# Local attention on Trainium2: weighing values or weighing tokens

## The chip, the cores and the metric

The kernel runs on one core of a Trainium2 chip. TensorE multiplies matrices and writes to PSUM; VectorE (DVE) and ScalarE (ACT) read PSUM; GpSimd (POOL) works on SBUF only; SyncE (SP) issues the transfers. Each engine takes its instructions in order, and they wait for one another by semaphores. The metric is the device time of one execution in microseconds (us). Everything is float32.

## The reference

A linear-attention block comes first (8 sequences of 512 tokens, width 128), then six layers of local attention and feed-forward. Cut to the layers and to what the change touches:

```python
def local_attention(q, k, v):              # 16 heads of 64, windows of 32 tokens
    bk2, bv2 = look(bk), look(bv)          # the previous window and the own one: 64 keys
    sim = einsum('bhwie,bhwje->bhwij', bq, bk2) * 8.0
    sim = where(mask, -max, sim)
    attn = softmax(sim, -1)
    return einsum('bhwij,bhwje->bhwie', attn, bv2)

def attn_layer(x, Wqkv, qs, ksc, Wo):
    q, k, v = split(x @ Wqkv, 3)           # v: 128 -> 16 heads x 64
    q, k = rotary(l2norm(q) * qs), rotary(l2norm(k) * ksc)
    return merge_heads(local_attention(q, k, v)) @ Wo

def ffn_layer(x, ...):
    a, gate = split(layernorm(x) @ W1 + b1, 2)     # 128 -> 2 x 341
    return a * gelu(gate) @ W2 + b2
```

For one head h, attn_h (x Wv_h) Wo_h equals (attn_h x) (Wv_h Wo_h). The kernel before computes the left side, the changed one the right side.

## The kernel before

The work of the six layers is cut into 192 units: 6 layers x 8 sequences x 4 blocks of 128 tokens. Each sequence is held as `state[b]`, 128 features by 512 tokens. The main loop (L766) runs over turns `t`. In turn `t` one unit enters, and older units do later steps; `at(t, lag, step)` calls a step for the unit that entered `lag` turns ago. With `ends=True` a step runs only for the last block of a sequence: this is how the feed-forward part, which works on 512 tokens at once, is put into every fourth turn. Four turns, one sequence of one layer, are called a batch below.

TensorE's order is the order in which the program is written (L757, `manual_schedule`). The orders of the other engines come out of a list scheduler, which takes what is ready on its own clock, prefers what stands under `tc.high_priority()`, and obeys `issue_behind(later, earlier)`, an order on one engine without a semaphore.

The steps of a unit:

- `proj` (L439), lag 0, for queries and for keys: two 128x512 products into a PSUM tile of tag "mm"; VectorE multiplies it by the rotary tables twice (`turned` L459, `straight` L467), ScalarE squares it (L475), GpSimd adds the two products (L482).
- `sum_squares` (L484) and `unit_length` (L491), lag 0: norms on VectorE, roots on ScalarE, scaling on GpSimd (L498).
- `values` and `spread` (L502 to L530), lag 0: the value product, a copy to SBUF, and up to ten transfers that lay the 64 values of each window out over the partitions.
- `by_features` (L532), lag 1: TensorE transposes queries and keys in four groups of four, each into a PSUM tile of tag "tr", which ScalarE copies out.
- `masked` (L553) and `scores` (L563), lag 1: ScalarE writes the mask to PSUM (tag "s"), 64 small products are added to it, VectorE takes the maxima (L580), ScalarE the 16 exponentials (L584), VectorE sums and reciprocals (L590, L591).
- `by_keys` (L594), lag 2: eight transposes of the weights and two copies. `weigh_values` (L604), lag 2: 64 small products with the values, then VectorE divides (L621).
- `out_by_features` (L627), lag 2: eight transposes and two copies (L635). `out_project` (L637), lag 3: eight products with Wo, and VectorE adds the result to `state` (L647).
- Feed-forward, at the ends: `feed_norm` (lag 3), `feed_first` (lag 4), `feed_middle` (lag 5, hidden products L667 and L669, gelu L673, product L675), `feed_last` (lag 6, L702, then L711).

[...] A new tile of a tag waits until all readers of the tile that held its buffer are done. Readers on two engines of the same PSUM tile run one after the other. `nc.tensor.addr_align` (L668 and L671, and in the loop) pads TensorE's instruction stream. The layer's weights are loaded by `load_layer` (L409) when its first unit enters.

Of the kernel before, what the change touches and what calls it, by code (L numbers as in the profile page):

```python
# [15 lines left out]
P = 128  # L16
# [7 lines left out]
FILL = 16  # L24
IN_STEP = 98
# [3 lines left out]
def sandwich_kernel(ctx: ExitStack, tc: tile.TileContext, ins: dict, out: bass.AP):  # L29
# [5 lines left out]
    DEPTH = ins["L0_ffn_Wqkv"].shape[0]  # L35
# [18 lines left out]
    state = [const.tile([P, N + 1], F32, tag=f"state_{b}", name=f"state_{b}") for b in range(B)]  # L54
    for b in range(B):
        nc.vector.memset(state[b][HD:P, 0:1], 0.0)
# [16 lines left out]
    tables, exps, divisions, copies, pcopies, maxima = [], [], [], [], [], []  # L73
# [7 lines left out]
    def gelu_only():  # L81
        ld = nc.scalar.preload_act_table_set("gelu_and_others")
        issue_behind(ld, pcopies[-1])
        issue_behind(ld, exps[-1])
        tables.append(ld)
# [67 lines left out]
    tw = wl.tile([P, 3, 2, 512], F32, tag="wqkv", name="tw")  # L153
# [4 lines left out]
    nc.sync.dma_start(tw[:, 2], a_w[:, 2])  # L158
# [3 lines left out]
    woT = tw[:, 2].rearrange("p s (c d) -> p (s c) d", d=DM)  # L162
# [246 lines left out]
    def load_layer(l):  # L409
        wqkv = wl.tile([P, 3, 2, 512], F32, tag="wqkv", name=f"wqkv_{l}")  # L410
        nc.sync.dma_start(
            wqkv, ins["L0_ffn_Wqkv"][l].rearrange("p (t s c) -> p t s c", t=3, s=2)
        )
        wo = wl.tile([P, NP, DM], F32, tag="wo", name=f"wo_{l}")
        nc.sync.dma_start(wo, ins["L0_ffn_Wo"][l].rearrange("(c p) d -> p c d", p=P))
# [21 lines left out]
        return dict(wqkv=wqkv, wo=wo, w1=w1, w2=w2, tab=tab)  # L437

    def proj(u, s):  # L439

        L, b, j = u["L"], u["b"], u["j"]
        wqkv, tab = L["wqkv"], L["tab"]
# [7 lines left out]
        for a in range(2):  # L450
            nc.tensor.matmul(  # L451
                ps[:, a].rearrange("p h d -> p (h d)"), lhs, wqkv[:, s, a, :], start=True, stop=True
            )
# [12 lines left out]
        def straight():  # L466
            nc.vector.tensor_tensor(  # L467
                t1, ps,
                tab[:, 2 * s, j, :].rearrange("p (a d) -> p a d", a=2).unsqueeze(2)
                .to_broadcast([P, 2, H, HF]),  # L470
                ALU.mult,
            )

        def squared(a):
            nc.scalar.activation(sq[:, :, a, :], ps[:, a], AF.Square)  # L475
# [8 lines left out]
    def sum_squares(u, s):  # L484
        su = nc.vector.tensor_reduce(  # L485
            u["ss"][:, s], u["sq", s].rearrange("p h a d -> p h (a d)"), AX.X, ALU.add
        )
        if divisions:
            issue_behind(su, divisions[-1])
# [12 lines left out]
    def values(u):  # L502
        L, b, j = u["L"], u["b"], u["j"]
        lhs = state[b][:, j * P : (j + 1) * P]

        v0 = f3.tile([P, 2, 512], F32, tag="v0", name="v0")
        ps = psum.tile([P, 2, 512], F32, tag="mm", name="mm")
        for p in range(2):
            nc.tensor.matmul(ps[:, p, :], lhs, L["wqkv"][:, 2, p, :], start=True, stop=True)  # L509
        u["v0"], u["v0ps"] = v0, ps  # L510

    def spread(u):
        j, v0 = u["j"], u["v0"]
        cp = nc.scalar.copy(v0, u.pop("v0ps"))
        if copies:
            issue_behind(cp, copies[-1])

        v2 = f2.tile([P, 4, 512], F32, tag="v2", name="v2")
        for p in range(2):
            if j == 0:  # L520
                nc.gpsimd.memset(v2[HD * p : HD * p + W, 0, :], 0.0)
            else:
                nc.sync.dma_start(v2[HD * p : HD * p + W, 0, :], u["B"]["v0"][P - W : P, p, :])
            nc.sync.dma_start(v2[HD * p + W : HD * (p + 1), 0, :], v0[0:W, p, :])
            for w in range(1, 4):
                nc.sync.dma_start(
                    v2[HD * p : HD * (p + 1), w, :], v0[W * (w - 1) : W * (w + 1), p, :]
                )
        u["B"]["v0"] = v0
        u["v2"] = v2  # L530
# [22 lines left out]
    def masked(u):  # L553
# [7 lines left out]
        issue_behind(sd, copies[-1])  # L561

    def scores(u):  # L563
# [24 lines left out]
        exps.append(ex)  # L588
        su = f2.tile([P, NP, 2], F32, tag="su", name="su")
        nc.vector.tensor_reduce(su, pe, AX.X, ALU.add)  # L590
        nc.vector.reciprocal(su, su)  # L591
        u["pe"], u["su"] = pe, su

    def by_keys(u):  # L594
        pe = u["pe"]
        u["pT"] = pT = f1.tile([P, NP, P], F32, tag="pT", name="pT")
        for c in range(0, NP, 4):
            ps = psum.tile([P, 4, P], F32, tag="tr", name="tr")
            for i in range(4):
                transposed(ps[:, i, :], pe[:, c + i].rearrange("p a k -> p (a k)"), P, P)  # L600
            with tc.high_priority():
                pcopies.append(nc.scalar.copy(pT[:, c : c + 4, :], ps))

    def weigh_values(u):  # L604


        v2, pT, su = u["v2"], u["pT"], u["su"]
        po = psum.tile([P, 2, NP, HD], F32, tag="s", name="po", bufs=1)
        for pair in range(NP):
            for w in range(4):  # L610
                for p in range(2):
                    r = slice(HD * p, HD * (p + 1))
                    nc.tensor.matmul(  # L613
                        po[W * w : W * (w + 1), p, pair, :],
                        pT[r, pair, W * w : W * (w + 1)],
                        v2[r, w, HD * pair : HD * (pair + 1)],
                        start=(pair == 0), stop=True, skip_group_check=True,
                    )
        u["on"] = on = f1.tile([P, NP, 2, HD], F32, tag="on", name="on")
        with tc.high_priority():  # L620
            dv = nc.vector.tensor_tensor(  # L621
                on.rearrange("t c p d -> t p c d"), po,
                su.rearrange("t c p -> t p c").unsqueeze(3).to_broadcast([P, 2, NP, HD]), ALU.mult,
            )
        divisions.append(dv)

    def out_by_features(u):  # L627
        on = u["on"]
        u["oT"] = oT = f1.tile([P, NP, P], F32, tag="oT", name="oT")
        for c in range(0, NP, 4):  # L630
            ps = psum.tile([P, 4, P], F32, tag="tr", name="tr")
            for i in range(4):
                transposed(ps[:, i, :], on[:, c + i].rearrange("p a d -> p (a d)"), P, P)
            with tc.high_priority():
                nc.scalar.copy(oT[:, c : c + 4, :], ps)  # L635

    def out_project(u):  # L637

        L, b, j, oT = u["L"], u["b"], u["j"], u["oT"]
        py = psum.tile([P, P], F32, tag="s", name="py", bufs=1)  # L640
        for c in range(NP):
            nc.tensor.matmul(py, L["wo"][:, c, :], oT[:, c, :], start=(c == 0), stop=(c == NP - 1))  # L642
# [7 lines left out]
    def feed_norm(u):  # L650
# [6 lines left out]
        u["normed"] = layer_norm(f2, xn, ps, NB, by_log=True, later=True)  # L657
# [4 lines left out]
    def feed_hidden(u, c):  # L662
# [5 lines left out]
        nc.tensor.addr_align(FILL, offset=FILL // 2)  # L668
        nc.tensor.matmul(pg[:cn, 1], w1[:, c0 : c0 + cn], xnT, start=True, stop=True)  # L669
        if c < NCH - 1:  # L670
            nc.tensor.addr_align(FILL, offset=FILL // 2)  # L671
# [85 lines left out]
    with tc.manual_schedule(engines={mybir.EngineType.PE}):  # L757
# [8 lines left out]
        for t in range(len(units) + 7):  # L766
            if t < len(units):
                u = units[t]
                if u["l"] not in layers:
                    layers[u["l"]] = load_layer(u["l"])  # L770
                u["L"] = layers[u["l"]]


            gelus = 0 <= t - 5 < len(units) and units[t - 5]["j"] == NB - 1
            at(t, 0, proj, 0)
            at(t, 0, proj, 1)


            if t % NB == 1 and NB < t < len(units):
                nc.tensor.addr_align(128, offset=IN_STEP)  # L780
            if t % NB == 3 and NB < t < len(units):
                nc.tensor.addr_align(FILL)
            at(t, 2, by_keys)
            if gelus:
                gelu_only()
            at(t, 3, out_project)
# [3 lines left out]
            if t == 1:  # L790
                attn_out(B - 1)
            at(t, 1, by_features, 0)
            at(t, 2, weigh_values)
            at(t, 1, by_features, 4, 0)
            at(t, 1, masked)
            at(t, 0, values)
# [6 lines left out]
            at(t, 1, by_features, 4, 1)  # L803
            at(t, 0, spread)
            at(t, 3, feed_norm, ends=True)
            at(t, 4, feed_first, ends=True)

            ends = 9 + NB * B * (DEPTH - 1) <= t < len(units) + 5
            after = 10 + NB * B * (DEPTH - 1) <= t < len(units) + 6
            if after:  # L810
                at(t, 10, out_roots, ends=True)
            if ends:
                at(t, 9, out_by_tokens, ends=True)
                at(t, 9, out_stats, ends=True)
            at(t, 5, feed_middle, ends=True)
            if gelus:
                at(t, 0, unit_length)
            at(t, 6, feed_last, ends=True)
            at(t, 1, scores)
            if after:  # L820
                at(t, 10, store, ends=True)
            if t == len(units) + 5:
                at(t, 6, out_by_tokens)
                at(t, 6, out_stats)
# [104 lines left out]
```

## Time and profile before

| | before |
|---|---|
| median of 3 runs | 3643.95 us (3640.91 to 3646.99) |
| span of the profiled execution (all that is given of its time) | 3641.2 us |
| first projection of the layers | at 478.96 us |
| last projection of the layers | at 3561.48 us |
| TensorE busy, granted clock | 98%, 0.993 |
| VectorE, ScalarE, GpSimd busy | 77%, 76%, 51% |

The span is the time from the first to the last instruction of one profiled execution. The first 479 us are the linear attention, which the change leaves as it is but for the tile that holds one of its weights. "Busy" counts the time in which an engine runs at least one instruction; matmuls overlap, and on the quarters of TensorE's rows several run at once, so TensorE's durations are best read from the distance between starts.

### The profile page before, as it was taken

To read this page: it belongs to the slowest core of one execution; us is meant where nothing else is said; L and a number is where in the kernel's file an instruction comes from. 1 tells how busy PE (TensorE), PEld (TensorE's weight loads), DVE (VectorE), ACT (ScalarE), POOL (GpSimd) and SP (SyncE) were. 2 spreads that over 40 slices of the span, in tenths; PEclk is the share of its full clock that TensorE was granted. 3 is DMA by queue.
4 is the path that set the end of the run, shared out by engine and by line. 5 is a ranking of instruction groups with operands and counts; after the bars stand their busy time and mean duration, and the time that the engine had idled before them with its cause. 6 is when DMAs were issued, how large, how long until landed. Compare 5 with 4: busy or idle time off the path is not lost.

```text
span 3641.2 us, 153034 instructions
## 1 busy us (share of the span) xinstructions
PE 3575.2 (98%) x65184; PEld 2404.3 (66%) x65184; DVE 2796.4 (77%) x3915; ACT 2765.6 (76%) x6864; POOL 1843.6 (51%) x1311
## 2 busy tenths in 40 slices
PE   8999989999999999999999999999999999999997
PEld 4555556666766666676766766667676676766765
DVE  4555567887878788787887878878787887878885
ACT  4555557787888888888787888888878787887875
POOL 0000045555655556555565655556555565556652
PEclk9999999999999999999999999999999999999998
DMA  3121132222232222232222322223222222222221
GB/s 109 46 53 47 42 89 68 65 65 69 79 77 72 65 64 71 77 81 68 61 69 68 87 72 69 65 65 86 71 71 69 60 70 64 66 68 73 74 74 47
DMA packets 158598, 250.73 MB, mean 69 GB/s; under 512 B 33774, under 2 KB 54508, under 8 KB 157164
## 3 DMA queue, kind: packets, MB, share of 16 engines
q1 hardware_dynamic: 157932, 240.93, 25.2%
q8 instruction: 530, 8.68, 1.0%
q14 instruction: 136, 1.11, 0.1%
HBM read 41.31 MB, written 4.46 MB: 13 GB/s over the span
## 4 chain that ended last, share of the span: by engine, by line
PE 87%; ACT 9%; DVE 2%; issue 1%; DMA 1%; POOL 0%; SPq 0%; POOLq 0%; DVEq 0%; ACTq 0%
PE tr L70 19%; PE mm L451 14%; PE py L642 10%; PE mm L509 9%; PE po L613 8%; PE sp L572 6%; ACT pe L584 4%; PE mm L667 4%; PE mm L669 4%; PE y L299 3%; PE py L702 3%; PE sc L269 2%; PE po L348 2%; ACT L76 1%; PE vv L247 1%; ACT oT L635 1%
## 5 line engine op out<-in xcount | busy, mean ns | idle before, releaser
L482 POOL TENSOR_TENSOR qk<-t,t 128x1024 f32<-128x1024 f32 x384 | 910.9, 2372 | 619.1 <-DVE t L467 424.7
L498 POOL TENSOR_TENSOR qk<-qk,ss 128x1024 f32<-128x1024 f32 x384 | 722.4, 1902 | 16.0
L451 PE MATMUL mm<-wqkv,state 128*128 128x512 f32 x1536 | 700.3, 596 | 0.6 <-issue 0.6
L584 ACT ACTIVATE pe<-sp,mx 128x64 f32<-128x64 f32 x3072 | 652.0, 381 | 2.4 <-DVE mx L580 2.3
L459 DVE TENSOR_TENSOR t<-mm,tab 128x1024 f32<-128x1024 f32 x384 | 468.3, 1219 | 220.3 <-PE mm L451 214.9
L475 ACT ACTIVATE sq<-mm 128x512 f32<-128x512 f32 x768 | 420.6, 605 | 127.4 <-DVE t L467 120.9
L467 DVE TENSOR_TENSOR t<-mm,tab 128x1024 f32<-128x1024 f32 x384 | 468.1, 1219 | 5.9
L451 PEld LDWEIGHTS mm<-wqkv,state 128*128 128x128 f32 x1536 | 273.1, 190 | 289.8 <-issue 242.4
L485 DVE TENSOR_REDUCE ss<-sq 128x16 f32<-128x1024 f32 x384 | 448.4, 1209 | 0.1
L70 PE MATMUL tr<-ident,qk 128*128 128x128 f32 x3072 | 440.9, 276 | 1.8 <-ACT qT L548 0.8
L70 PEld LDWEIGHTS tr<-ident,qk 128*128 128x128 f32 x3072 | 351.3, 141 | 120.7 <-issue 56.3
L642 PE MATMUL py<-oT,wo 128*128 128x128 f32 x3072 | 379.3, 277 | 0.3 <-ACT oT L635 0.3
L642 PEld LDWEIGHTS py<-oT,wo 128*128 128x128 f32 x3072 | 368.1, 196 | 0.5 <-ACT oT L635 0.5
L509 PE MATMUL mm<-wqkv,state 128*128 128x512 f32 x768 | 362.9, 595 | 2.6 <-DVE t L467 2.6
L635 ACT COPY oT<-tr 128x512 f32<-128x512 f32 x384 | 205.5, 587 | 168.1 <-PE tr L70 165.5
L572 PEld LDWEIGHTS sp<-kT,qT 64*32 64x32 f32 x24576 | 264.2, 105 | 91.3 <-issue 54.3
L613 PE MATMUL po<-v,pT 64*32 64x64 f32 x24576 | 297.0, 225 | 9.6 <-issue 3.9
L548 ACT COPY qT<-tr 128x512 f32<-128x512 f32 x384 | 226.3, 589 | 99.6 <-PE tr L70 99.1
L613 PEld LDWEIGHTS po<-v,pT 64*32 64x32 f32 x24576 | 268.8, 105 | 46.0 <-PE tr L70 24.6
L572 PE MATMUL sp<-kT,qT 64*32 64x64 f32 x24576 | 297.6, 225 | 0.3 <-issue 0.3
L495 POOL TENSOR_SCALAR ss<-ss 128x32 f32<-128x32 f32 x192 | 54.7, 285 | 478.7 <-ACT ss L98 470.8
L548 ACT COPY kT<-tr 128x512 f32<-128x512 f32 x384 | 225.6, 588 | 74.8 <-PE tr L70 74.5
(110 smaller groups left out, 5243.9 us busy)
## 6 DMA issues: line engine op xcount, KB each, us to landing
v<-v SPq DMA_DIRECT2D x1152, 128.0 KB
v<-v SPq DMA_DIRECT2D x672, 64.0 KB
rs<-roots SPq DMA_DIRECT2D x64, 256.0 KB
wqkv<-in_L_ffn_Wqkv_dram SPq DMA_DIRECT2D x6, 1536.0 KB
wo<-in_L_ffn_Wo_dram SPq DMA_DIRECT2D x6, 512.0 KB
xin<-_attn_hidden_states_dram SPq DMA_DIRECT2D x8, 256.0 KB
xr<-_attn_hidden_states_dram SPq DMA_DIRECT2D x8, 256.0 KB
x<-xr SPq DMA_DIRECT2D x8, 256.0 KB
```

What stands on the lines that cost most here:

```text
L70: nc.tensor.transpose(ps[:cols, :rows], src, ident[:rows, :rows])
L451: nc.tensor.matmul(ps[:, a].rearrange("p h d -> p (h d)"), lhs, wqkv[:, s, a, :], start=True, stop=True)
L459: nc.vector.tensor_tensor(t2, ps[:, ::-1], tab[:, 2 * s + 1, j, :].rearrange("p (a d) -> p a d", a=2).unsqueeze(2) .to_broadcast([P, 2, H, ...
L467: nc.vector.tensor_tensor(t1, ps, tab[:, 2 * s, j, :].rearrange("p (a d) -> p a d", a=2).unsqueeze(2) .to_broadcast([P, 2, H, HF]), ALU.mult,)
L482: nc.gpsimd.tensor_tensor(qk[:, s].rearrange("p h a d -> p a h d"), t1, t2, ALU.add)
L498: nc.gpsimd.tensor_tensor(t, t, ss[:, i, :].unsqueeze(2).to_broadcast([P, H, HD]), ALU.mult)
L509: nc.tensor.matmul(ps[:, p, :], lhs, L["wqkv"][:, 2, p, :], start=True, stop=True)
L548: copies.append(nc.scalar.copy(dst, ps))
L572: nc.tensor.matmul(sp[W * w : W * (w + 1), p, pair, :], qT[HD * p : HD * (p + 1), pair, W * w : W * (w + 1)], kT[HD * p : HD * (p + 1), pa ...
L584: ex = nc.scalar.activation(pe[:, pair, p, :], sp[:, p, pair, :], AF.Exp, bias=mx[:, p, pair : pair + 1])
L613: nc.tensor.matmul(po[W * w : W * (w + 1), p, pair, :], pT[r, pair, W * w : W * (w + 1)], v2[r, w, HD * pair : HD * (pair + 1)], start=(pa ...
L642: nc.tensor.matmul(py, L["wo"][:, c, :], oT[:, c, :], start=(c == 0), stop=(c == NP - 1))
```

## The change

The values are never computed. Once a layer, the products Wv_h Wo_h are made for the 16 heads (`value_products`: 16 products of 64 rows, kept as `wm`). The host lays the weights out for this (`Wqk` and `Wvo` in place of `Wqkv` and `Wo`). For a unit:

- `by_tokens` (lag 2) transposes two 128-token windows of `state`, one shifted back by 32 tokens, and ScalarE copies them out. For this the state gets 32 columns of zeros in front.
- `divided` (lag 2): sums and reciprocals as before, but the weights themselves are divided, by GpSimd.
- `by_keys` (lag 3) is one VectorE transpose in 32x32 blocks, of 128x1024.
- `weigh_tokens` (lag 3): eight products of 32 rows by 512 columns, on four quarters of TensorE's rows, into two "mm" tiles, and two ScalarE copies of 128x1024.
- `out_project` (lag 4): 16 products in place of eight, into a "tr" tile in place of "s".

Everything behind it moves by one turn. The padding of the instruction stream goes, the loads of the next layer are issued half a layer ahead, `feed_norm` copies its transposes to SBUF before the statistics, and some orders on ScalarE and VectorE are written differently. The core of the diff:

```diff
-        wqkv = wl.tile([P, 3, 2, 512], F32, tag="wqkv", name=f"wqkv_{l}")
...
+        wqk = wl.tile([P, 2, 2, 512], F32, tag="wqk", name=f"wqk_{l}")
+        nc.sync.dma_start(wqk, ins["L0_ffn_Wqk"][l].rearrange("p (t s c) -> p t s c", t=2, s=2))
...
+    def value_weights(l):
+
+        wv = f1.tile([P, NP, DM], F32, tag="on", name="wv")
+        wo = f1.tile([P, NP, DM], F32, tag="oT", name="wo")
+        for s, t in enumerate((wv, wo)):
+            nc.sync.dma_start(t.rearrange("p c d -> p (c d)"), ins["L0_ffn_Wvo"][l, s])
+        wm = wl.tile([P, 2, NP, DM], F32, tag="wm", name=f"wm_{l}")
+        layers[l].update(wv=wv, wo=wo, wm=wm)
+
+    def value_products(l):
+        L = layers[l]
+        for c in range(0, NP, 4):
+            ps = psum.tile([P, 2, 4, DM], F32, tag="mm", name="wm")
+            for i in range(4):
+                for p in range(2):
+                    r = slice(HD * p, HD * (p + 1))
+                    nc.tensor.matmul(
+                        ps[:, p, i, :], L["wv"][r, c + i, :], L["wo"][r, c + i, :], start=True, stop=True,
+                        skip_group_check=True,
+                    )
+            nc.scalar.copy(L["wm"][:, :, c : c + 4, :], ps)
...
+    def by_tokens(u):
+
+        b, j = u["b"], u["j"]
+        ps = psum.tile([P, 2, P], F32, tag="tr", name="tx")
+        for a in range(2):
+            c0 = j * P + a * W
+            transposed(ps[:, a, :], wide[b][:, c0 : c0 + P], P, P)
+        u["x"] = x = f2.tile([P, 2, P], F32, tag="x", name="x")
+        nc.scalar.copy(x, ps)
...
         issue_behind(sd, copies[-1])
+        issue_behind(sd, squared_last[-1])
...
+    def divided(u):
+        pe = u["pe"]
         su = f2.tile([P, NP, 2], F32, tag="su", name="su")
-        nc.vector.tensor_reduce(su, pe, AX.X, ALU.add)
+        sm = nc.vector.tensor_reduce(su, pe, AX.X, ALU.add)
+        if turns:
+            issue_behind(sm, turns[-1])
         nc.vector.reciprocal(su, su)
-        u["pe"], u["su"] = pe, su
+        nc.gpsimd.tensor_tensor(pe, pe, su.unsqueeze(3).to_broadcast([P, NP, 2, 2 * W]), ALU.mult)
 
     def by_keys(u):
...
+        u["pT"] = pT = f1.tile([P, H, 2, W], F32, tag="pT", name="pT")
+        turned = nc.vector.transpose(
+            pT.rearrange("k h a t -> k (h a t)"), u["pe"].rearrange("t c p k -> t (c p k)")
+        )
+        issue_behind(turned, straights[-1])
+        turns.append(turned)
+
+    def weigh_tokens(u):
+
+        x, pT = u["x"], u["pT"]
+        ps = [psum.tile([P, 2, H, W], F32, tag="mm", name="z") for _ in range(2)]
+        for a in range(2):
             for w in range(4):
...
+                r = slice(W * w, W * (w + 1))
+                nc.tensor.matmul(
+                    ps[w // 2][:, w % 2], x[r, a, :], pT[r, :, a, :], start=(a == 0), stop=(a == 1),
+                    skip_group_check=True,
+                )
+        u["zT"] = zT = f2.tile([P, H, 4, W], F32, tag="v2", name="zT")
+        for i in range(2):
+            nc.scalar.copy(zT[:, :, 2 * i : 2 * i + 2, :].rearrange("f h w t -> f w h t"), ps[i])
 
     def out_project(u):
...
+        L, b, j, zT = u["L"], u["b"], u["j"], u["zT"]
+        py = psum.tile([P, P], F32, tag="tr", name="py")
+        for h in range(H):
+            nc.tensor.matmul(
+                py, L["wm"][:, h % 2, h // 2, :], zT[:, h].rearrange("f w t -> f (w t)"),
+                start=(h == 0), stop=(h == H - 1),
+            )
...
         u["xn"] = xn = f1.tile([P, NB, DM], F32, tag="xn", name="xn")
-        u["normed"] = layer_norm(f2, xn, ps, NB, by_log=True, later=True)
+        nc.scalar.copy(xn, ps)
+        u["normed"] = layer_norm(f2, xn, xn, NB, by_log=True, later=True)
```

The main loop after the change, with the steps of the first block and the output left out:

```python
at(t, 0, proj, 0); at(t, 0, proj, 1)
at(t, 3, by_keys); at(t, 2, divided)
if gelus: gelu_only()
at(t, 4, out_project)
if t == 2: value_products(0)
at(t, 1, by_features, 0)
at(t, 2, by_tokens)
at(t, 1, by_features, 4, 0); at(t, 1, by_features, 4, 1)
at(t, 1, masked)
at(t, 0, sum_squares, 0); at(t, 0, sum_squares, 1)
if not gelus: at(t, 0, unit_length)
at(t, 4, feed_norm, ends=True); at(t, 5, feed_first, ends=True)
if t % (NB * B) == NB * B - 3: value_products(u["l"] + 1)
at(t, 6, feed_middle, ends=True)
if gelus: at(t, 0, unit_length)
at(t, 7, feed_last, ends=True)
at(t, 3, weigh_tokens)
at(t, 1, scores)
at(t, 4, feed_normed, ends=True)
```

## The prediction

> **What bounds the kernel now.** I read the page's busy shares and chain first, then TensorE in order of time over four turns of the main loop, then VectorE and ScalarE at the places that the change moves.
>
> ```profile
> span 3641.2 us, 153034 instructions
> PE 3575.2 (98%) x65184; PEld 2404.3 (66%) x65184; DVE 2796.4 (77%) x3915; ACT 2765.6 (76%) x6864; POOL 1843.6 (51%) x1311
> ...
> PE 87%; ACT 9%; DVE 2%; issue 1%; DMA 1%; POOL 0%; SPq 0%; POOLq 0%; DVEq 0%; ACTq 0%
> ```
>
> TensorE has work all the time and carries 87% of the chain. The next view is TensorE in order of time (start, duration, line); a turn (one unit of 128 tokens enters) begins at each L451 row.
>
> ```profile
> 154.08 1.14 PE L269 MATMUL sc<-tq,tk 32*128 32x512 f32 x8
> 155.15 7.41 PE L348 MATMUL po<-tw,yT 128*128 128x128 f32 x64
> ...
> 1999.80 3.60 PE L451 MATMUL mm<-wqkv,state 128*128 128x512 f32 x8
> 2003.24 1.06 PE L70 MATMUL tr<-ident,pe 128*128 128x128 f32 x8
> 2004.14 1.95 PE L642 MATMUL py<-oT,wo 128*128 128x128 f32 x16
> 2005.92 1.04 PE L70 MATMUL tr<-ident,qk 128*128 128x128 f32 x8
> 2007.01 1.48 PE L613 MATMUL po<-v,pT 64*32 64x64 f32 x128
> ...
> 2013.93 3.79 PE L451 MATMUL mm<-wqkv,state 128*128 128x512 f32 x8
> ...
> 2028.17 3.60 PE L451 MATMUL mm<-wqkv,state 128*128 128x512 f32 x8
> ...
> 2045.08 1.58 PE L572 MATMUL sp<-kT,qT 64*32 64x64 f32 x128
> ...
> 2047.52 3.60 PE L451 MATMUL mm<-wqkv,state 128*128 128x512 f32 x8
> ...
> 2061.73 1.63 PE L572 MATMUL sp<-kT,qT 64*32 64x64 f32 x128
> ...
> 2064.22 2.31 PE L451 MATMUL mm<-wqkv,state 128*128 128x512 f32 x5
> ```
>
> The four turns take 14.13, 14.24, 19.35 (the feed-forward's hidden products) and 16.70 us (its last product): 64.42 for four units, 48 times over. A 128x512 product is two instructions: 3.44/8 = 0.43 us each; 128x128 ones take 0.112 (1.79/16), transposes 0.109. The first two rows matter most: eight 32-row instructions of 512 columns, on four quarters of the rows, pass in 1.07 us, not in 8 x 0.43.
>
> Last, VectorE and ScalarE near what moves.
>
> ```profile
> 2020.45 0.58 DVE L647 TENSOR_TENSOR state<-py,state 64x128 f32<-64x128 f32 x2
> 2022.61 1.08 ACT L475 ACTIVATE sq<-mm 128x512 f32<-128x512 f32 x2 [0.66 <-DVE t L467]
> 2045.19 0.68 ACT L673 ACTIVATE ge<-mm,vec 85x512 f32<-85x512 f32 x1 [1.12 <-PE mm L669]
> 2045.90 0.75 DVE L675 SCALAR_TENSOR_TENSOR gT<-mm,vec,ge 85x512 f32<-85x512 f32 x1 [1.05 <-ACT ge L673]
> 2061.84 1.52 DVE L711 SCALAR_TENSOR_TENSOR state<-py,vec,state 64x512 f32<-64x512 f32 x2 [1.85 <-PE py L702]
> ```
>
> See that the squares wait for VectorE's second product of the same PSUM tile, and that a feed-forward "mm" tile is read to the end only at 2046.65 (1.57 us after TensorE left it at 2045.08) and at 2063.36 (1.63 after 2061.73). Today nobody wants these buffers then.
>
> **TensorE's sum.** Removed per unit: value products 4 x 0.43 = 1.72, 8 transposes of weights 0.88, 64 small products 1.48, 8 transposes of outputs 0.93: 5.0. Added: 8 products of 32 rows by 512 columns, 16 instructions in two groups of the L269 kind, 4 x 0.43 + 0.1 for the first weights = 1.85; 16 more output instructions 1.79; two transposes 0.22: 3.86. A plain turn's TensorE work becomes 3.44 + 3.57 + 0.87 + 0.22 + 0.87 + 1.85 + 1.41 = 12.2, from some 13.8. If that were the turn, 192 x 1.15 to 1.5 us would go. So the question is what TensorE waits for.
>
> **The turn by waits.** Clock 0 is the first projection; durations are rows' (VectorE's 128x1024 operations start 1.13 apart, first at 1.99; 128x512 copies 0.59; exponentials 3.4 from 1.45).
> - VectorE: four products 1.99 to 6.52, then the new turn of the weights, ordered behind them. No row shows that operation. Lower end 0.68 (the 128x512 copy, L251), upper 2.45 (two 128x1024 operations). I take 1.13, as its 128x1024 neighbours.
> - The output product ends at 7.01 and its adds into the state can start at 7.23. As in the row at 2020.45 they start at the first gap after that: 7.65 to 8.23, behind the turn.
> - The output product now sits in one of the two "tr" banks. The key transposes (second group of q0, k0, tokens, q4, k4) want it back, or the q0 copy at 8.28 (squares until 7.70 first): they start at 8.25, not 7.45. From there two banks and ScalarE's copies take turns: k0 copied 9.44, tokens 9.84 (0.4 us for 128x256), q4 transposed 9.90 and copied 10.65, k4 transposed 10.34 and copied 11.24, mask 11.24 to 12.26. Today other products lie between these groups.
> - Weighing 10.34 to 12.2, scores 12.3 (mask) to 13.75. The new copies of 128x1024 (1.02 each, L514) run 12.73 to 14.77, behind the roots; the next projections need the buffers at 13.75 and 15.5: hidden by scores and the first projection; without that cover up to 2 us.
> Plain turn: 13.75 against 14.1; of 1.6 us saved 1.2 is lost.
>
> The feed-forward turns lose more, because weighing takes both "mm" buffers directly behind a feed-forward step, and its second half (quarters 2 and 3) waits for the reader of that step's last tile:
> - hidden products: 10.34 + 5.54 (2039.54 to 2045.08) + 1.57 + 1.75 + 1.45 = 20.65 (was 19.35);
> - last product: 10.34 + 2.67 + 1.63 + 1.75 + 1.45 = 17.85 (was 16.70);
> - norm: transposes to 10.8, the new copy of 0.59 behind the k4 copy, 11.24 to 11.83, then 1.75 + 1.45: 15.05 (was 14.13). The data are there at 10.95, so I put this copy before the mask; after it, 1.05 more, 50 us in all;
> - first: waits for the q4 copy, 10.7 + 0.43 + 1.85 + 1.45 = 14.45 (was 14.24).
> Sum 68.0 against 64.42: +3.6 x 48 = +173 us.
>
> [...]
>
> **The rest.** Products of value and output weights: 32 instructions a layer, 1.8 us, then two copies of 1.02 that the hidden products' buffers wait for: some 2.5 us x 6 = 15. One more stage drains at the end: half a plain turn, 6 (bounds 0 and 14). The division moves to GpSimd (1.9 us, L498): some 11.0 of 13.75 us there, and the weights are wanted a turn later: nothing; uncovered 1.9. SP loses 1824 spread transfers and gets 12 weight loads half a layer early, for the spread nobody waits any more: nothing. The six table products of 3.2 us move with the loads to mid-layer, beside GpSimd's 11: under 1 us, five times. ScalarE drops 3.2 us of copies and gains 2.4: in the clock above. Dropped instruction padding: the chain has 1% "issue", so between -36 and +36; taken 0, since TensorE issues 202 instead of 316 products a unit. Sum: 3641.2 + 173 + 21 = 3835 for the profiled execution (only its span is given); the median lies 2.75 above that span, so 3838.
>
> **Rivals.**
> 1. The adds get in before the turn (7.23): all from the k0 group is 0.45 earlier, 66.1 a batch, +80 + 21: 3745. Against it: VectorE would have to sit idle from 6.52.
> 2. Faster: the buffers don't bind, because the orders that come out for VectorE and ScalarE empty them sooner than I lay out. TensorE alone needs 4 x 12.2 + 9.1 = 57.9 a batch; with 1 us of waits a turn 61.9, -2.5 x 48 + 21: 3545. It decides once waits fall under 6.1 us a batch; I count 10. For it: TensorE's own work falls by a tenth. Against: the two readers' 1.57 and 1.63 and the mask's 1.02 stand in the rows.
> 3. The turn of the weights takes 2.45: adds and everything after 1.15 later, 192 x 1.1 = 211: 4050.
> 4. The quarters don't overlap: 6.9 for 1.85, +970: 4810. The L269 rows speak against it.
> 5. No change: the waits come to the 6.1 us a batch at which gain and loss cancel.
>
> **How the numbers follow.** Main case 0.42 (own range 3780 to 3900: the norm's order, +50, and the padding), rival 1 0.20, rival 2 0.20, rival 3 0.13, rival 4 0.02, rival 5 0.03. Runs differ by 6 us in 3644, so under 0.2% (7 us) is no change. Faster 0.20, same 0.03, slower 0.77. The range from 3550 to 4010 leaves out half of rival 2, most of rival 3's upper half and rival 4.
>
> **What would show it.** Right: TensorE's busy share drops while ScalarE and VectorE are named as releasers before the qk transposes, the weighing and the scores; hidden turns near 20.6; weighing in about 1.85 where nothing stalls it. Wrong: plain turns near 12.5, weighing that doesn't wait behind L675's and L711's successors, or a weights' turn far from 1.13.

## The result

| | time, us (median) | ratio to the kernel before |
|---|---|---|
| before | 3643.5 (3640.9 to 3647.0) | |
| predicted | 3838 (3550 to 4010) | 1.053 |
| after | 4014.4 (4010.7 to 4018.9) | 1.102 [1.101, 1.104] |

The direction was right, the size was not: 371 us lost instead of 195, 4 us outside the range. The page of the changed kernel: span, busy time by engine, the chain that ended last by engine, and two of its groups (busy us, mean ns, then TensorE's idle time in front of them and who ended it).

```profile
span 4008.7 us, 101718 instructions
PE 3573.7 (89%) x43488; PEld 2258.0 (56%) x43488; DVE 2741.1 (68%) x3923; ACT 2666.6 (67%) x6540; POOL 2143.8 (53%) x1407
...
PE 47%; ACT 20%; DVE 19%; issue 7%; POOL 6%; DMA 1%; SPq 0%; ACTq 0%; DVEq 0%; POOLq 0%
...
L70 PE MATMUL tr<-ident,qk 128*128 128x128 f32 x3072 | 448.2, 279 | 278.4 <-ACT qT L545 183.0
L613 PE MATMUL z<-pT,x 32*128 32x512 f32 x3072 | 542.0, 624 | 84.9 <-ACT xn L644 31.2
```

A third of the instructions are gone and TensorE is busy for the same 3574 us. Busy doesn't mean in full use: the same instructions in another order (experiment 1) make 3422 us, since a weighing cut in two by a wait counts as busy while half of TensorE's rows are unused (the weighing's own rows are 542 us here and 385 there). TensorE now idles for 11% of the span, and its share of the chain fell from 87% to 47%. Two groups carry the idle time: 278 us before the key and query transposes (1.8 before the change) and 85 us before the weighing. ScalarE and VectorE end them, as the prediction said they would.

The next view is TensorE in order of time (start, duration, line; in brackets the idle time just before a row and what ended it). It has the turn of the hidden products, the second half of the last product's turn, and the turn of the norm; a turn begins at each L469 row.

```profile
2217.15 3.70 PE L469 MATMUL mm<-wqk,state 128*128 128x512 f32 x8
2220.68 3.73 PE L626 MATMUL py<-zT,wm 128*128 128x128 f32 x32
2224.26 0.60 PE L70 MATMUL tr<-ident,qk 128*128 128x128 f32 x4
2226.03 0.63 PE L70 MATMUL tr<-ident,qk 128*128 128x128 f32 x4 [1.18 <-ACT qT L545]
2226.50 0.38 PE L70 MATMUL tx<-ident,state 128*128 128x128 f32 x2
2227.39 1.09 PE L70 MATMUL tr<-ident,qk 128*128 128x128 f32 x8 [0.51 <-ACT kT L545]
2228.32 1.02 PE L655 MATMUL mm<-xnT,w 128*128 128x512 f32 x2
...
2233.64 1.13 PE L613 MATMUL z<-pT,x 32*128 32x512 f32 x4
2235.27 1.99 PE L613 MATMUL z<-pT,x 32*128 32x512 f32 x12 [0.50 <-DVE gT L660]
2237.19 1.48 PE L570 MATMUL sp<-kT,qT 64*32 64x64 f32 x128
2238.60 3.70 PE L469 MATMUL mm<-wqk,state 128*128 128x512 f32 x8
...
2253.79 1.99 PE L613 MATMUL z<-pT,x 32*128 32x512 f32 x12 [0.65 <-DVE state L696]
...
2257.11 3.70 PE L469 MATMUL mm<-wqk,state 128*128 128x512 f32 x8
...
2270.23 1.99 PE L613 MATMUL z<-pT,x 32*128 32x512 f32 x12 [0.66 <-ACT xn L644]
```

Read it as the prediction's clock: key transposes start 8.88 us into the hidden turn (8.25 forecast), the second group at 10.24 (by the forecast it is half done at 9.90), and the second half of the weighing waits behind the late reader in all three turns, named as forecast (successors of L675 and L711, and the new copy xn). The first L613 row has four instructions, the two quarters whose buffer is free; its 1.13 us is what the eight instructions of the L269 row (1.14) need on all four quarters. So half of it is lost, though the row counts as busy.

VectorE and ScalarE of the hidden turn, in order of time:

```profile
2222.64 1.21 DVE L485 TENSOR_TENSOR t<-mm,tab 128x1024 f32<-128x1024 f32 x1
2223.77 1.23 DVE L600 STREAM_TRANSPOSE pT<-pe 128x1024 f32<-128x1024 f32 x1
2224.93 0.55 DVE L634 TENSOR_TENSOR state<-py,state 64x128 f32<-64x128 f32 x2
```

```profile
2221.81 1.20 ACT L494 ACTIVATE sq<-mm 128x512 f32<-128x512 f32 x2
2223.03 1.28 ACT L82 ACT_TABLE_LOAD   x1
2224.32 1.08 ACT L494 ACTIVATE sq<-mm 128x512 f32<-128x512 f32 x2
2225.30 0.59 ACT L545 COPY qT<-tr 128x512 f32<-128x512 f32 x1
```

The adds into the state stand behind the turn of the weights, as in the main case. ScalarE's squares of a tile start behind VectorE's second product of it, by 0.03 us or more in all 384 tiles of either kernel. The load of gelu's table stands between the squares and pushes the copy of q0 back, to 2225.89; the k0 transposes start 0.14 us behind it. The prediction's clock did not have that load.

Median turns in the main loop, for every kernel of this study (us; the runs are explained below):

| kernel | first | hidden | last | norm | sum | time |
|---|---|---|---|---|---|---|
| before | 14.24 | 19.29 | 16.69 | 14.13 | 64.35 | 3643 |
| predicted | 14.45 | 20.65 | 17.85 | 15.05 | 68.0 | 3838 |
| after | 15.30 | 21.45 | 18.51 | 16.45 | 71.71 | 4014 |
| weighing first | 14.71 | 19.47 | 16.83 | 14.99 | 66.00 | 3731 |
| gelu's load later | 15.30 | 22.23 | 18.51 | 16.45 | 72.49 | 4050 |
| normalisation later | 16.91 | 21.21 | 18.51 | 16.45 | 73.08 | 4072 |
| padding back | 15.30 | 22.46 | 18.51 | 16.45 | 72.72 | 4094 |
| tokens early | 14.85 | 20.56 | 18.05 | 15.88 | 69.34 | 3897 |
| adds first | 15.03 | 20.56 | 18.05 | 15.93 | 69.57 | 3908 |
| weighing first, tokens early | 14.51 | 19.05 | 16.33 | 14.31 | 64.20 | 3654 |
| the same, adds first | 14.52 | 18.83 | 17.09 | 15.43 | 65.87 | 3731 |
| the same, roots later | 15.41 | 18.73 | 16.18 | 14.29 | 64.61 | 3687 |
| weighing between | 13.84 | 20.01 | 16.28 | 14.45 | 64.58 | 3667 |
| gelu's load behind the mask | 13.84 | 19.38 | 16.28 | 14.45 | 63.95 | 3645 |
| shift on ScalarE | 13.84 | 18.90 | 16.28 | 14.45 | 63.47 | 3625 |

The spans differ by 367.5 us. The sum of four turns, 7.36 us longer, gives 338.6 over the 46 batches behind the first eight turns; the drain gives 7.1; turns outside the pattern give 28.8, among them 2.85 us in the one turn of each layer that has the products of value and output weights, and some 0.9 in turns of the last layer. The first eight turns are 4.6 us shorter, 2.2 go off for the last turn, which the drain already holds, and the first projection comes 0.2 earlier.

### The profile page after: what moved, and what is told of

Read it like the earlier page. It is cut to its first block, busy times and chain, and to the rows that moved or that the text cites. A ratio compares the mean times of both kernels' runs of the same rounds, so it can differ in the third digit from the quotient of the medians.

```text
span 4008.7 us, 101718 instructions
## 1 busy us (share of the span) xinstructions
PE 3573.7 (89%) x43488; PEld 2258.0 (56%) x43488; DVE 2741.1 (68%) x3923; ACT 2666.6 (67%) x6540; POOL 2143.8 (53%) x1407
## 4 chain that ended last, share of the span: by engine, by line
PE 47%; ACT 20%; DVE 19%; issue 7%; POOL 6%; DMA 1%; SPq 0%; ACTq 0%; DVEq 0%; POOLq 0%
PE z L613 9%; PE tr L70 8%; DVE t L477 7%; PE sp L570 7%; POOL qk L501 6%; ACT sq L494 5%; DVE t L485 5%; PE mm L469 5%; ACT kT L545 4%; ACT pe L582 3%; ACT qT L545 3%; PE mm L655 3%; PE mm L656 3%; PE y L299 3%; PE py L687 3%
## 5 line engine op out<-in xcount | busy, mean ns | idle before, releaser
L626 PEld LDWEIGHTS py<-zT,wm 128*128 128x128 f32 x6144 | 715.9, 192 | 95.1 <-issue 89.9
L626 PE MATMUL py<-zT,wm 128*128 128x128 f32 x6144 | 717.4, 275 | 3.2 <-ACT zT L619 3.2
L469 PE MATMUL mm<-wqk,state 128*128 128x512 f32 x1536 | 712.9, 607 | 3.9 <-DVE t L485 2.6
L578 DVE TENSOR_REDUCE mx<-sp 128x16 f32<-128x1024 f32 x192 | 235.0, 1224 | 570.2 <-PE sp L570 570.0
L613 PE MATMUL z<-pT,x 32*128 32x512 f32 x3072 | 542.0, 624 | 84.9 <-ACT xn L644 31.2
L596 POOL TENSOR_TENSOR pe<-pe,su 128x1024 f32<-128x1024 f32 x192 | 365.3, 1903 | 339.8 <-DVE su L595 335.7
L70 PEld LDWEIGHTS tr<-ident,qk 128*128 128x128 f32 x3072 | 337.2, 141 | 364.7 <-issue 222.3
L619 ACT COPY zT<-z 128x1024 f32<-128x1024 f32 x384 | 369.2, 1013 | 219.7 <-PE z L613 219.3
L469 PEld LDWEIGHTS mm<-wqk,state 128*128 128x128 f32 x1536 | 277.0, 190 | 299.7 <-issue 277.7
L613 PEld LDWEIGHTS z<-pT,x 32*128 32x128 f32 x3072 | 181.7, 184 | 375.6 <-issue 205.4
```

Of the source, the lines that this page charges most:

```text
L70: nc.tensor.transpose(ps[:cols, :rows], src, ident[:rows, :rows])
L469: nc.tensor.matmul(ps[:, a].rearrange("p h d -> p (h d)"), lhs, wqk[:, s, a, :], start=True, stop=True)
L613: nc.tensor.matmul(ps[w // 2][:, w % 2], x[r, a, :], pT[r, :, a, :], start=(a == 0), stop=(a == 1), skip_group_check=True,)
L626: nc.tensor.matmul(py, L["wm"][:, h % 2, h // 2, :], zT[:, h].rearrange("f w t -> f (w t)"), start=(h == 0), stop=(h == H - 1),)
```

## The experiments

Theory A: TensorE waits for PSUM buffers ("tr" behind the adds and ScalarE's copies, "mm" behind the feed-forward readers; the program keeps two of each, "tr" of up to 128x512 and "mm" of up to 128x1024, and one "s" of 128x1024) because of where the steps stand in the turn. Theory B: the dropped instruction padding costs the time. Theory C: TensorE's own new work, above all the 32 instructions of the output product, costs it.

**1. The weighing and the scores ahead of the feed-forward steps.** The exponentials, split off from `scores` as `weights`, stay behind these steps.

```diff
+            at(t, 3, weigh_tokens)
+            at(t, 1, scores)
             at(t, 4, feed_norm, ends=True)
...
-            at(t, 3, weigh_tokens)
-            at(t, 1, scores)
+            at(t, 1, weights)
```

> In TensorE's order, weighing and scores come before the feed-forward steps (the exponentials stay behind them). Theory A (TensorE waits for PSUM buffers that late readers hold, above all the "mm" tiles of the feed-forward steps in front of weighing): the turns of 15.30, 21.45, 18.51 and 16.45 us become 15.3, 19.8, 16.7 and 14.6, since weighing takes 1.9 in place of 3.6 to 3.7; 5.3 less a batch, some 247 in all, about 3765 us. Theory B (the dropped padding of the instruction stream costs the time) and theory C (TensorE's own work, the 16 output products, sets the time): no change, 4014 us.

Measured: 3731.2, ratio 1.025 [1.023, 1.026]; 283 of the 371 us are back. TensorE in order of time, the hidden turn of this kernel:

```profile
2079.82 3.61 PE L469 MATMUL mm<-wqk,state 128*128 128x512 f32 x8
...
2088.24 0.63 PE L70 MATMUL tr<-ident,qk 128*128 128x128 f32 x4 [0.80 <-ACT qT L545]
...
2089.60 1.09 PE L70 MATMUL tr<-ident,qk 128*128 128x128 f32 x8 [0.51 <-ACT kT L545]
2090.62 2.00 PE L617 MATMUL z<-pT,x 32*128 32x512 f32 x16
2092.55 1.48 PE L570 MATMUL sp<-kT,qT 64*32 64x64 f32 x128
```

The weighing passes whole, in 1.93 us to the next row, and every feed-forward turn falls by 1.5 to 2.0 us. In the hidden turn 0.4 of it is not the weighing's: gelu's table load has come to stand ahead of the squares in this kernel, and the wait before k0 is 0.80 for 1.18. TensorE does exactly the same work here, so C can't explain these 283 us; it is not excluded for the other 88. What stays are the two waits in front of the second and third group of transposes, 1.3 us a turn.

**2. Gelu's table load behind the copy of k4**, out of the squares (one ordering on ScalarE, the call moved behind the key transposes and ahead of the mask's).

```diff
         issue_behind(ld, exps[-1])
+        issue_behind(ld, copies[-1])
```

> The load of the gelu table goes behind the last copy of the keys, instead of between the two squares. Theory A: in the turn with the hidden products the first key transposes start 0.5 earlier (8.35 for 8.88 after the turn's start), 21.45 becomes 20.95, 24 us in all: about 3990 us. Theories B and C: 4014 us.

Measured: 4050.2, ratio 1.112 [1.111, 1.114]: 36 us worse. The wait before k0 fell from 1.18 to 0.80 as meant, but ScalarE, then TensorE (two views of this kernel) show where it went:

```profile
2249.26 1.28 ACT L82 ACT_TABLE_LOAD   x1
2250.55 1.27 ACT L659 ACTIVATE ge<-mm,vec 128x512 f32<-128x512 f32 x2
```

```profile
2252.08 1.09 PE L656 MATMUL mm<-xnT,w 128*85 128x512 f32 x2 [1.00 <-DVE gT L661]
```

The load now stands directly before the first gelu, and the third chunk of hidden products waits 1.00 us for the buffer of the first. A miss for my theory of this one wait: 0.78 us a batch lost where 0.5 was to be won.

**3. The normalisation of the tokens behind the turn of the weights** (`feed_normed` waits for `turns[-1]`, not for the maxima).

> The normalisation of the feed-forward input (four operations, 1.8 us) goes from the start of the next turn, in front of the rotary products, to behind the turn of the weights. Theory A: the turn of 15.30 becomes 14.4, the others stay, 43 us in all: about 3970 us. Theories B and C: 4014 us.

Measured: 4072.1, ratio 1.118 [1.116, 1.120]: 58 us worse. VectorE, ScalarE and TensorE in order of time:

```profile
2237.29 2.35 DVE L111 TENSOR_SCALAR xn<-xn,ln_mv,ln_rs 128x128 f32<-128x128 f32 x3
2239.56 1.21 DVE L504 TENSOR_REDUCE ss<-sq 128x16 f32<-128x1024 f32 x1
```

```profile
2242.83 0.23 ACT L95 ACTIVATE ss<-ss 128x32 f32<-128x32 f32 x1 [2.92 <-DVE ss L504]
...
2243.23 1.91 ACT L619 COPY zT<-z 128x1024 f32<-128x1024 f32 x2
```

```profile
2244.28 3.70 PE L469 MATMUL mm<-wqk,state 128*128 128x512 f32 x8 [0.91 <-ACT zT L619]
```

Of the three normalising operations in the first row the last takes 1.93 us, beside GpSimd's division (see experiment 9), and the sums of squares stand behind it. The late sums of squares hold the roots, the roots stand in ScalarE's queue ahead of the copies of zT, and the next projection waits for those. This is the uncovered copy that the prediction priced at "up to 2 us": its cover is only as good as the queue ahead of it.

**4. The instruction padding put back** where the program of the kernel before has it: within the hidden products and behind the projections of two turns in four. As every step now stands a turn later, these two are the turns of the hidden products and of the norm; they were those of the last product and of xn's transposes ("first").

```diff
+        nc.tensor.addr_align(FILL, offset=FILL // 2)
         nc.tensor.matmul(pg[:cn, 1], w1[:, c0 : c0 + cn], xnT, start=True, stop=True)
...
+            if t % NB == 1 and NB < t < len(units):
+                nc.tensor.addr_align(128, offset=IN_STEP)
```

> The padding of TensorE's instruction stream is put back at the same places. Theory B: at least half of what the sum missed comes back, 90 us, under 3925 us. Theories A and C: 4014 us within 20.

Measured: 4093.5, ratio 1.124 [1.122, 1.126]: 79 us worse, so B falls for the padding as it was put back; other places were not tried. TensorE in order of time, in two hidden turns of this kernel:

```profile
2266.32 6.33 PE L628 MATMUL py<-zT,wm 128*128 128x128 f32 x32 [5.80 <-issue]
...
2341.51 3.81 PE L628 MATMUL py<-zT,wm 128*128 128x128 f32 x32 [1.13 <-issue]
```

TensorE waits for nothing that the profile shows ("issue"): 1.1 to 1.3 us in nearly every hidden turn, and once a layer 5.80 with a slow row behind it (that turn is 6.3 to 7.4 us over the median, five times).

**5. The tokens' transposes ahead of the output product.** Then the two "tr" buffers pass tx, py, q0, k0, q4, k4.

```diff
+            at(t, 2, by_tokens)
             at(t, 3, by_keys)
...
-            at(t, 2, by_tokens)
```

> The changed kernel with one step moved: the two transposes of the token states (tx) are issued ahead of the output product instead of between the key transposes. The two tr buffers then pass tx, py, q0, k0, q4, k4, so that the second group no longer waits for the tokens' copy between k0 and q4. Theory A (TensorE waits for tr and mm buffers that late readers hold): k4 ends about 0.6 us earlier in every turn, 192 x 0.6 = 115 us, so about 3900 (3870 to 3940). A milder form of A: the tokens' copy (0.38 us) now stands among the squares on ScalarE and makes the copy of q0 as much later, which leaves 0.2 us a turn: 3975. Theory C (TensorE's own longer output product costs the time): the same instructions, so 4014 +- 15.

Measured: 3897.4, ratio 1.070 [1.068, 1.071]: 117 us, as expected. TensorE in order of time, in the turn of the last product:

```profile
2187.93 1.06 PE L70 MATMUL tr<-ident,qk 128*128 128x128 f32 x8 [0.56 <-DVE state L634]
2189.23 0.66 PE L70 MATMUL tr<-ident,qk 128*128 128x128 f32 x4 [0.24 <-ACT kT L545]
```

The second wait falls from 0.51 to 0.24 us, and each turn by 0.45 to 0.9. About half of the gain was not worked out beforehand: in three of the four turns the first wait is now ended by the adds, at 0.56 us, where the copy of q0 ended it at 0.80 (at 1.18 in the hidden turn, behind gelu's table load). That the sum came out so close is in part luck.

**6. Adds ahead of the turn of the weights, on the changed kernel alone**, with the sums of squares ordered behind the turn. It is the prediction's rival 1, made.

> The changed kernel with that order of VectorE alone: adds, turn of the weights, sums. The prediction's rival 1 puts 0.45 us a turn on it, about 90 us: 3925. If the copy of q0 ends at the same time as the adds, as the trace of the changed kernel has it (both near +8.35), nothing is gained: 4014 +- 20.

Measured: 3908.4, ratio 1.073 [1.072, 1.075]: 106 us, where rival 1 had put 93 and I, after reading the trace of the changed kernel, nothing. The hidden turn alone gives 0.89 us of the 2.14 a batch: k0 no longer waits for the copy that gelu's table load pushes back there, which rival 1 had not counted. VectorE, ScalarE and TensorE of one turn:

```profile
2196.07 0.59 DVE L638 TENSOR_TENSOR state<-py,state 64x128 f32<-64x128 f32 x2 [0.60 <-PE py L630]
2196.69 1.25 DVE L602 STREAM_TRANSPOSE pT<-pe 128x1024 f32<-128x1024 f32 x1
```

```profile
2196.53 0.59 ACT L547 COPY qT<-tr 128x512 f32<-128x512 f32 x1
```

```profile
2196.81 0.63 PE L70 MATMUL tr<-ident,qk 128*128 128x128 f32 x4 [0.34 <-DVE state L638]
```

The k0 transposes start 0.15 us behind the adds (2196.66), while the copy of q0 still runs until 2197.12. In the changed kernel they start 0.14 to 0.15 us behind that copy in all four turns of the batch shown. Both are true, because the two tiles have changed buffers: in the changed kernel's program the k0 transposes wait on ScalarE (q0's buffer) and the tokens' transposes on VectorE (the output product's), in this one it is the other way round. With the adds issued early, k0 takes the buffer that the output product leaves and no longer the one behind it. I had read the wait's end off the trace and held the buffers for fixed.

**7 and 8. Both moves together, then the adds on top.**

> The weighing and scores ahead of the feed-forward steps (the first experiment) and the tokens' transposes ahead of the output product together. Theory A: the two waits are in different buffers (mm and tr) and add up: 3731 - 115 = 3616, which would be below the kernel before (3641). If the tokens' copy delays the copy of q0: 3690. Theory C: 3731 +- 15.

> As the run before, and the adds into the state are ordered ahead of VectorE's turn of the weights, the sums of squares behind it. The adds then end at about +7.8 instead of +8.35 us. If they alone hold k0's buffer, 0.4 us a turn, 75 us: about 3540. If the copy of q0 on ScalarE holds the other buffer just as long: no change, within 15 us of the run before. Theory C: no change.

Measured: 3654.3, ratio 1.003 [1.002, 1.004], for weighing and tokens; 3731.4, 1.024 [1.023, 1.026], with the adds on top. The first pair add up to 77 of the expected 115 us. The adds, worth 106 us alone, cost 77 here. ScalarE and TensorE of that run:

```profile
1845.38 0.23 ACT L95 ACTIVATE ss<-ss 128x32 f32<-128x32 f32 x1 [1.19 <-DVE ss L504]
...
1845.78 1.91 ACT L627 COPY zT<-z 128x1024 f32<-128x1024 f32 x2
```

```profile
1846.83 2.84 PE L695 MATMUL py<-gT,w 128*128 128x512 f32 x6 [0.83 <-ACT zT L627]
```

It is the mechanism of experiment 3: with the turns this tight, sums 1.1 us later are late for the roots, and these stand in front of zT.

**9. The same, and the roots behind zT on ScalarE.**

> As the run with the adds ahead of the turn on top of weighing and tokens moved, and on ScalarE the roots of the sums of squares are ordered behind the two copies of zT instead of ahead of them. Theory A, from that run's trace: the sums end about 1.1 us later there, the roots wait for them and hold up the copies of zT, and TensorE waits 0.83 us for an mm buffer in two turns of four. Behind the copies the roots hold up nobody: those waits go, 0.8 + 1.1 us a batch, 47 batches, 90 us, so 3640. If the cost is the later turn of the weights itself: no change, 3731 +- 15.

Measured: 3686.8, ratio 1.013 [1.011, 1.015]: half the expected gain. The two turns with those waits fall to 16.18 and 14.29, by 0.9 and 1.1 us where 0.8 and 1.1 were worked out, which confirms the queue; the first turn rose by 0.89 us. VectorE and GpSimd there:

```profile
1776.40 1.65 DVE L113 TENSOR_SCALAR xn<-xn,ln_mv,ln_rs 128x128 f32<-128x128 f32 x1
```

```profile
1775.82 1.90 POOL L519 TENSOR_TENSOR qk<-qk,ss 128x1024 f32<-128x1024 f32 x1
```

Later roots start GpSimd's products later, which now run beside VectorE's normalisation. The first of its four operations takes 1.65 us, until 0.33 behind the end of GpSimd's product (1777.72); the other three take 0.33 to 0.39, as all four did in the run before. So this operation was not slow throughout: it ended one operation's own time behind GpSimd's, as if it had stood still until then.

**10 to 12. The weighing between the key transposes.** The order becomes q0, weighing, k0, q4, k4, scores, so that TensorE works while the adds end; the mask stands behind the copy of q0, zT behind that of k4, the roots behind zT, normalisation and adds behind the turn of the weights. Then gelu's load behind the mask; then scale and shift of xnT on ScalarE.

```diff
-            at(t, 1, by_features, 0)
+            at(t, 1, by_features, 0, 0)
+            at(t, 1, masked)
+            at(t, 3, weigh_tokens)
+            at(t, 1, by_features, 0, 1)
             at(t, 1, by_features, 4, 0)
             at(t, 1, by_features, 4, 1)
...
+            at(t, 3, z_copies)
             at(t, 1, scores)
```

> As the run with weighing and tokens moved; the weighing now stands between the first and the second group of key transposes, where TensorE waits for the adds; the mask is taken behind the copy of q0, the copies of zT behind that of k4, the roots behind zT, the normalisation and the adds behind VectorE's turn of the weights. Theory A: TensorE has 1.93 us of work while the adds end, and the remaining 0.5 + 0.24 us a turn go; a plain turn becomes TensorE's own 12.44 us plus about 0.5 instead of 14.3, some 60 us a batch for 64.2, so 3460 (3430 to 3560). If the copies of zT and the mask on ScalarE, or GpSimd's 11 us a turn, bind next, up to nothing is won: 3650. Theory C: 3654 +- 15.

> As the run with the weighing between the key transposes, and the load of gelu's table on ScalarE moved from between the squares to behind the mask, where that run's trace has ScalarE idle for 1.32 us. Theory A: in that run the load (1.28 us) delays the squares of k, these hold the second mm buffer, and the weighing stalls within (2.63 us for 2.00), once a batch; with it gone the turn of the hidden products falls from 20.01 to some 18.8, 47 times: 3667 - 56 = 3611, below the kernel before (3642). If the load now delays the copy of k0 by as much: no change, 3667 +- 15.

> As the run before, and the scale and shift of the normalised tokens (xnT, 0.81 us on VectorE, ahead of the rotary products of the hidden products' turn) is done by ScalarE behind the copies of zT. Theory A: VectorE's products, and with them the turn of the weights, come 0.6 us earlier in that turn, and the 0.66 us for which the weighing waits for pT goes, 47 times: 3645 - 30 = 3615, below the kernel before (3641). If ScalarE's exponentials are pushed back and the squares hold the mm buffer in its place: no change, 3645 +- 10.

Measured: 3667.4, 1.007 [1.006, 1.008]; 3645.1, 1.001 [1.000, 1.002]; 3625.1, 0.995 [0.994, 0.997]. TensorE in order of time, the hidden turn of the last of them:

```profile
1763.84 3.60 PE L472 MATMUL mm<-wqk,state 128*128 128x512 f32 x8
...
1771.07 0.60 PE L70 MATMUL tr<-ident,qk 128*128 128x128 f32 x4
1771.75 2.00 PE L621 MATMUL z<-pT,x 32*128 32x512 f32 x16
1773.68 1.09 PE L70 MATMUL tr<-ident,qk 128*128 128x128 f32 x8
1775.16 0.66 PE L70 MATMUL tr<-ident,qk 128*128 128x128 f32 x4 [0.39 <-ACT kT L548]
```

The wait for the adds is gone. All three fell short. Gelu's load brought 22 us of the 56 expected (the hidden turn came to 19.38, not 18.8), the shift 20 of 30. The first was far from its 3460: its norm turn has two waits left, 0.29 and 0.26 us, and yet takes 14.45; less these and the 0.66 us of the norm's transposes, TensorE's own plain turn, restarts included, is some 13.2 us and not the 12.44 that I had summed. The last kernel is 17 us faster than the kernel before: with its steps placed where TensorE waits less, the changed kernel gains 0.5%, and it lost 10% where they stood. The gain is not all the idea's, as far as is known: gelu's load and the shift were not moved in the kernel before.

## Where the prediction was right and where it failed

**Right.** The sign and its mechanism: buffers emptied late outweigh TensorE's saving, and the main case's order on VectorE (four products, turn of the weights, adds, sums) came out exactly. Quarters overlap: the unstalled weighing takes 1.93 us against 1.85, so rival 4 (6.9) is out. The turn of the weights takes 1.23 us, and the adds start 1.16 us behind its start, for which 1.13 was taken; rival 3 (2.45) is out. The two new copies behind the weighing are covered, as the main case took them: they take 1.91 to 1.93 us, as long as the weighing, and in the whole span TensorE idles 0.9 us for them before the projections and 3.2 us before the output product. What costs is other tiles' readers in the same buffers, 278 us before the key and query transposes and 85 us before the weighing. The padding was rightly taken as no gain. The drain, forecast at 6, is 7.1 us. (The 202 and 316 "products" a unit are instructions.)

**The step that failed: the sum of the four turns, 68.0 for 71.7 measured.** The waits came where the prediction put them; what was mis-sized is the clock between them. By that clock, in us a batch:

| term | missed by | what the trace has |
|---|---|---|
| start of key and query transposes, all four turns | 4 x 0.40 | projection 3.54 for 3.44, and about 0.15 from each release to TensorE's next instruction, twice a turn |
| norm: the new copy behind the mask | 0.9 | the mask first; I had named this order, priced it at 1.05 and taken the other |
| restart of the weighing behind a late reader | 0.7 | 1.92 us from the restart to the scores for 1.75, and up to 0.15 from the reader's end to the restart, in three turns |
| hidden: gelu's table load | 0.4 | between the squares; not on the clock |
| first: normalisation ahead of the rotary products, xn's transposes | 0.45 | 0.18 and 0.27; not on the clock |
| hidden products | -0.2 | 5.32 for 5.54 |

No term is large. The largest is the start of the transposes: the two-buffer ping-pong was laid out with 0.02 us between a release and TensorE's next start (8.23 to 8.25), the rows have about 0.15. And nearly all errors of the clock have one sign, because each wait starts behind the one before. Over 46 batches 3.7 us make 170 of the 176 us missed; turns outside the pattern, 29 us for the 15 forecast, outweigh the shorter first turns.

**The rivals.** Rival 1's order did not come out by itself, but made in experiment 6 it is worth 106 us for the 93 that it said. In the changed kernel it was the copy of q0, the other of the two releases that the prediction named, that held k0, as late as the adds or later. Rival 2's turning point, 6.1 us of waits a batch, was too kind. With the weighing first, the waits that remain are 5.1 us and the kernel is still slower, because TensorE is busy for 60.86 us of a batch there and not for 57.9:

```profile
2079.82:2145.81 65.99, 60.86 (x836) 40.13 (x835) 50.72 (x67) 49.93 (x129) 43.78 (x29) 1.00 0.01 2
```

(The view of busy time by stretch, for one batch: length, then PE, PEld, VectorE, ScalarE, GpSimd.) Against 64.25 in the kernel before, the change frees 3.4 us a batch there and not the 6.3 that I had counted. Groups cut off by waits take longer than in an unbroken stream (in the view of experiment 1, 0.63 for four transposes and 1.02 from the start of eight to the next row, where 0.44 and 0.87 were summed). With these restarts the change could give 3.4 x 48, some 160 us, before any idle time, and not 300.

**The range** kept the norm's other order and rival 3 as separate ends and added up nothing; several small delays of one sign were not in it.

## What to carry to other kernels

When a change takes work from the bounding engine, write down first who empties each buffer and how long after the engine leaves it; then move the new work to a place where its buffers are already free, before judging the idea: the same products cost 10% in one order and gained 0.5% in another, with two smaller moves besides. In a clock of two buffers add a latency for each hand-over (here about 0.15 us) and every instruction that shares the reader's queue, table loads (here 1.28 us) and normalisations (0.33 to 1.93 us an operation) too. A wait's releaser in the profile says which buffer a tile got in this order of steps, not which it would get in another.

## What the runs showed that I had not expected

- Padding of TensorE's instructions, put where the program before had it, cost 1.1 to 1.3 us of "issue" in nearly every hidden turn of the changed stream and once a layer 6 to 7 us: 79 us in all.
- VectorE's normalisation (128x128 operations, SBUF to SBUF) was held up by a GpSimd product that was already running. In experiment 9 that befell 47 of the 192, which took 1.3 to 1.8 us and nearly all ended 0.33 us behind the product; the other 145 took 0.33 to 0.39. In the changed kernel four ran beside such a product; they took 1.24 to 1.26 us and each ended 0.33 us behind it, the other 188 took 0.33 to 0.39. VectorE's 128x1024 products of a PSUM tile took 1.21 to 1.23 us there, the 396 that ran beside GpSimd's products as well as the 372 that did not. GpSimd's operations read and write SBUF in every row of both traces. In the kernel before, the normalisation reads PSUM, and 188 of its 192 operations ran beside GpSimd's products, none held up (the view gives the shortest, the median and the longest in ns):

```profile
L112 DVE TENSOR_SCALAR xn<-nx,ln_mv,ln_rs x192: 397/402/409, 597.7 to 3617.1; 128x128 f32<-128x128 f32 x192
```

  So by these traces the copy to SBUF that the change puts in front of the statistics also exposes the normalisation to GpSimd; no run changed the source alone.
- One reordering is worth +106 us or -77 us, depending on what else has been moved: the adds ahead of the turn of the weights pay while the "tr" buffers bind, and cost once the roots in front of zT do.
